# Float8 rounding in units 6 and 7 of a chunk, and the float8 product in unit 0 of the next, in a fused attention block

## The chip, the cores and the metric

The kernel runs on one core of a Trainium2 chip, as a single launch. The metric is device time in microseconds (us), lower is better. The core has a matrix engine (PE, whose weight loads are shown as PEld), a vector engine (DVE), a scalar engine (ACT), a general engine (POOL) and a queue that issues DMAs (SP). Each engine works through its own instructions in order and waits on semaphores for the others.

## What is computed

The input is `x`, 4 batches of 1024 tokens of 512 values, all in float32. It is normalized, and the result is the input plus an attention block plus a small product in float8:

```python
xn = _layernorm(x)
x = x + attention(xn, ...) + ffn(xn, input2, scale, scale1)

# ffn
q1 = (xn * scale).astype(float8_e4m3fn)
q2 = (input2 * scale1).astype(float8_e4m3fn)
out = (q1.astype(float32) / scale) @ (q2.astype(float32) / scale1)

# attention: 16 heads of 128
q = rope(rmsnorm(xn @ Wq + bq)); lk = rope(rmsnorm(xn @ Wlk + blk)); lv = xn @ Wlv + blv
entries = weighted mean of each 4 tokens of xn         # 256 per batch
ck = rope(rmsnorm(entries @ Wk + bk)); cv = entries @ Wv + bv
sparse = softmax over the 8 best of q . ck, times cv    # causal
local  = softmax of q . lk over the 128 tokens before and itself, times lv
out = ((sparse + local) / 2) @ Wo + bo
```

The change touches only when the float8 part `ffn(xn, ...)` is computed.

## The kernel before

**Tiles.** The tokens are cut into 32 chunks of 128 (`t`, 0 to 31; `c = t mod 8` is the chunk's place in its batch). The 16 heads of a chunk are worked in 8 units of two heads (`u`, 0 to 7). The main loop (L791) runs over steps `s = 8 t + u` and in each step works on several units at once: scores and softmax of unit s, queries and keys of unit s + 3, values' projection of unit s + 1, the context of unit s - 1 and the output projection of unit s - 2. The order of every instruction on every engine is the order of the code: it is written by hand, and no scheduler changes it.

**One step on PE** (the order in which it meets its work): `scores` of unit s for two heads (sc, L572 to L583), `queries` (qp, L445 and L446), what the chunk work adds in its first call (below), `to_output` (op, L753), `values_of` (vp, L537), `values` (cp, L720). A little of a name's meaning: qp holds raw queries and keys, th the normalized and rotated ones (L467, L309 to L312), vp the raw values, which ACT copies to lv (L549), prob the softmax weights, which DVE (L661) and DMAs (pr, then probT, L703) transpose.

**One step on DVE**: `weigh` and `settle` of unit s (L605 to L638), the chunk work of the first call, the chunk work of the second call, the add of the output when a chunk ends (L762, in unit 1 of the next chunk), `turn` (L661), `normalize` (L467, L310 to L312), `turn_keys` (L512, L515). On POOL: the chunk work of the first call, the reciprocal root r (L290, L291), the chunk work of the second call, and rb (L309).

**Chunk work** is done by generators, of which each step takes two pieces: the function `steps()` (L768) calls `next` once on every generator in the list `running`, and the main loop calls it twice a step, first after `settle` (L812), then after `to_output` (L818).

- `chunk_prep(t + 2)` (L318) starts in u = 7 of chunk t and takes 18 pieces, nine steps: layernorm (L329 to L337: statistics in unit 7, xn in unit 0), its transposition on PE (xp, L342, unit 1), the projection yp (L352, unit 2), the entries ep (L382, unit 4), kv (unit 5), its scaling and rotation on DVE and POOL (L404, then L309 to L312 for 32 entries, unit 6), the transposition cp on PE (L412) in the first call of unit 7, and its copy to ckT on DVE (L414) in the second call of unit 7. The scores of the next chunk read ckT (L582).
- `chunk_eight(t)` (L417) is the float8 part in six pieces. Piece 1: three DVE operations on 128 x 512 (L262, L263, L266) and a POOL add (L267). Pieces 2 to 4: one POOL operation each (L269, L271, L273), the last of which writes x8. Piece 5: the product on PE, four bfloat16 matmuls into fp (L425). Piece 6: DVE scales fp and adds the bias (f, L430), and POOL adds f to x_sum (L431). In unit 1 of the next chunk L762 adds the attention's output to x_sum, and SP stores it (L763).

In the kernel before, `chunk_eight(t)` starts in u = 5: pieces 1 and 2 in unit 5, pieces 3 and 4 in unit 6, pieces 5 and 6 in unit 7.

**Shared buffers.** All these PSUM tiles come from one tag, `pp`, with two buffers in turn: vp of every unit, and xp, yp, ep, cp and fp of the chunk work. A tile can be written only when the last reader of the tile two before it in the order of the code is done. In unit 7 that order is cp, fp, vp. In the same way xn, y, qv, qm and f share two buffers named `scratch`, and the inputs x two buffers.

## Time and profile before

| | |
|---|---|
| time, median of 3 runs | 2831.97 us (2831.59 to 2832.27) |
| the profiled execution | 2833.53 us, its span 2831.6 us |
| granted PE clock, mean | 0.997 |
| HBM traffic | 140 GB/s over the span |
| one chunk, by the starts of vp | some 80 to 94 us, longer with c |

Share of the span is how long an engine was busy. A matmul's end is modelled and matmuls overlap, so the busy time of PE isn't the time of its stream; the starts of its groups are. In the timeline each line has the start and the length in us, the engine, the line of the code, the operation, what is written and read, the shape and how many of them, and in brackets the idle time just before and what ended it.

The chunk work of the float8 part, with its counts and mean lengths:

```profile
L262 DVE TENSOR_SCALAR qv_x<-xnT,scales 128x512 f32<-128x512 f32 x32 | 15.3, 479 | 0.0
L263 DVE TENSOR_SCALAR qm_x<-qv_x 128x512 uint32<-128x512 uint32 x32 | 13.7, 427 | 1.1
L266 DVE TENSOR_SCALAR qm_x<-qm_x 128x512 f32<-128x512 f32 x32 | 13.7, 427 | 1.1
L267 POOL TENSOR_TENSOR qv_x<-qv_x,qm_x 128x512 f32<-128x512 f32 x32 | 40.7, 1273 | 34.2 <-DVE qm_x L266 34.2
L425 PE MATMUL fp<-w_sb,x 128*128 128x512 bf16 x127 | 32.9, 381 | 0.1
```

The columns after the bar are the busy time in us, the mean length of one in ns, and the idle time before them with what ended it.

### The profile page before, as it was taken

Reading aid. Unit: us, or ns where it says so; the run is one execution under the profiler, and the core shown is the slowest. Engines: PE = TensorE matmul, PEld = TensorE weight load, DVE = VectorE, ACT = ScalarE, POOL = GpSimd, SP = SyncE. Lnnn points to the kernel's source line nnn. Section 1 sums busy time; section 2 is a strip of 40 time slices with the busy share of each in tenths; the row PEclk is TensorE's granted clock in tenths of the full one; section 3 lists DMA queues with packets and bytes.
Section 4 is the critical chain, followed back from the end, with each engine's and each line's share of the span. In section 5 each row is a group of like instructions: output and inputs, shape, how many; then the busy total and the mean of one; then the engine's idle time right before and its main releaser. Section 6 shows DMA issues by size and latency. Waiting matters only on the chain. (4 is left out here: it accounts for less than half of the span.)

```text
span 2831.6 us, 48506 instructions
## 1 busy us (share of the span) xinstructions
PE 2769.0 (98%) x12771; PEld 1873.8 (66%) x12969; DVE 2247.1 (79%) x9132; ACT 1299.1 (46%) x5075; POOL 821.3 (29%) x1161
## 2 busy tenths in 40 slices
PE   6999999999999999999999999999999999999998
PEld 4666666666666666666666666666666666667666
DVE  5777888888777778888877787888887777888886
ACT  3445444444444454444444444444444444444443
POOL 3432232322233322233223333223222233322221
PEclk9999999999999999999999999999999999999999
DMA  7345455555445445555544444555554544555553
GB/s 230 90 138 138 133 143 152 144 150 153 127 124 139 137 133 152 144 151 149 149 126 131 134 135 134 155 148 149 146 149 122 135 136 131 136 152 155 143 149 108
DMA packets 620850, 399.85 MB, mean 141 GB/s; under 512 B 306880, under 2 KB 573984, under 8 KB 620576
## 3 DMA queue, kind: packets, MB, share of 16 engines
q1 hardware_dynamic: 608352, 383.18, 48.8%
q10 hardware_dynamic: 12224, 13.56, 1.5%
q8 instruction: 105, 1.72, 0.3%
q14 instruction: 169, 1.38, 0.2%
HBM read 212.53 MB, written 184.03 MB: 140 GB/s over the span
## 5 line engine op out<-in xcount | busy, mean ns | idle before, releaser
L445 PE MATMUL qp<-wqk,xnT 128*128 128x512 f32 x2048 | 945.5, 604 | 4.9 <-DMA scales<-in_L_ffn_scale_dram 3.3
L445 PEld LDWEIGHTS qp<-wqk,xnT 128*128 128x128 f32 x2048 | 370.6, 191 | 385.2 <-issue 371.5
L612 ACT ACTIVATE prob<-sc,neg 128x256 f32<-128x256 f32 (+1 forms) x512 | 236.0, 461 | 779.6 <-DVE taken L611 759.3
L537 PEld LDWEIGHTS vp<-wlv,xnT 128*128 128x128 f32 x2048 | 386.5, 190 | 188.7 <-issue 94.0
L537 PE MATMUL vp<-wlv,xnT 128*128 128x256 f32 x2048 | 487.0, 381 | 17.2 <-DVE ckT L414 11.9
L753 PE MATMUL op<-wo,cT 128*128 128x512 f32 x1024 | 484.9, 596 | 7.1 <-ACT cT L735 1.5
L290 POOL TENSOR_SCALAR r<-ss 128x4 f32<-128x4 f32 x256 | 49.8, 194 | 1067.3 <-ACT junk L296 1059.3
L661 DVE STREAM_TRANSPOSE probB<-prob 128x512 f32<-128x512 f32 (+2 forms) x494 | 282.4, 609 | 92.5 <-ACT prob L643 89.1
L467 DVE SCALAR_TENSOR_TENSOR th<-qp,r,norm_w 128x128 f32<-128x128 f32 x1024 | 283.6, 339 | 71.0 <-POOL r L291 70.2
L309 POOL TENSOR_TENSOR rb<-th,cs 128x256 f32<-128x256 f32 x256 | 247.0, 965 | 278.0 <-DVE th L467 277.9
L296 ACT ACTIVATE junk<-qp 128x128 bf16<-128x128 f32 x1024 | 284.1, 277 | 88.0 <-remote 42.7
L549 ACT COPY lv<-vp 128x256 f32<-128x256 f32 x256 | 95.5, 373 | 477.6 <-PE cp L720 420.0
L753 PEld LDWEIGHTS op<-wo,cT 128*128 128x128 f32 x1024 | 188.9, 190 | 188.4 <-issue 113.9
L720 PE MATMUL cp<-probT,lv 128*128 128x128 f32 x1920 | 299.4, 276 | 4.4 <-DMA probT<-pr 4.4
L720 PEld LDWEIGHTS cp<-probT,lv 128*128 128x128 f32 x1920 | 276.1, 193 | 18.1 <-issue 5.2
L291 POOL TENSOR_TENSOR r<-r,nhalf 128x4 f32<-128x4 f32 x256 | 259.6, 1014 | 21.4
L720 PE MATMUL cp<-probT,cv 128*128 128x128 f32 x1536 | 256.7, 276 | 0.0
L582 PE MATMUL sc<-ckT,qT 128*128 128x96 f32 (+7 forms) x1024 | 226.5, 303 | 0.0
L643 ACT ACTIVATE prob<-prob,tot 128x256 f32<-128x256 f32 (+1 forms) x512 | 223.0, 484 | 3.6 <-DVE tot L637 3.6
L720 PEld LDWEIGHTS cp<-probT,cv 128*128 128x128 f32 x1536 | 214.3, 193 | 0.0
L605 DVE CUSTOM_DVE_ANT_0 sc<-sc,mask_b 128x256 f32<-128x256 f32 (+1 forms) x512 | 202.6, 396 | 7.2 <-PE sc L583 6.6
L579 PE MATMUL sc<-lkT,qT 128*128 128x128 f32 x1024 | 207.8, 285 | 0.0
(123 smaller groups left out, 3858.3 us busy)
## 6 DMA issues: line engine op xcount, KB each, us to landing
pr<-probB SPq DMA_DIRECT2D x127, 512.0 KB, 2.6
probT<-pr SPq DMA_DIRECT2D x508, 128.0 KB, 2.9
qk<-thb SPq DMA_DIRECT2D x992, 64.0 KB, 2.0
pr<-probB SPq DMA_DIRECT2D x96, 384.0 KB, 2.6
probT<-pr SPq DMA_DIRECT2D x384, 96.0 KB, 2.4
qT<-qk SPq DMA_DIRECT2D x248, 128.0 KB, 2.3
lkT<-qk SPq DMA_DIRECT2D x248, 128.0 KB, 2.5
x_norm<-_attn_hidden_states_dram SPq DMA_DIRECT2D x32, 256.0 KB, 3.2
```

What stands on the lines that cost most here:

```text
L291: nc.gpsimd.tensor_tensor(r, r, nhalf[: ss.shape[0], 0:n], ALU.pow)
L296: nc.scalar.activation(junk[: src.shape[0]], src, AF.Square, accum_out=acc)
L309: nc.gpsimd.tensor_tensor(bb, x12, wide(cs[:, HALF:ROPE]), ALU.mult)
L445: nc.tensor.matmul(qp, xnT[:, k, :], wqk_sb[u][:, k, :], start=(k == 0), stop=False)
L467: nc.vector.scalar_tensor_tensor(th[:, i, :], qp[:, ts(i, D)], r[:, i : i + 1], norm_w[:, i // 2, :], ALU.mult, ALU.mult,)
L537: nc.tensor.matmul(vp[:, 0:256], xnT[:, k, :], wlv_sb[u][:, k, :], start=(k == 0), stop=(k == KK - 1),)
L582: nc.tensor.matmul(sc[:, spa], q, ckT[:, 0:m], start=True, stop=False)
L612: nc.scalar.activation(prob[:, loc], sc[:, loc], AF.Exp, bias=neg[:, 0:1], scale=-1.0, accum_out=tot[:, 0:1],)
L643: nc.scalar.mul(prob[:, loc], prob[:, loc], tot[:, 0:1])
L661: nc.vector.transpose(pb[:, :, ds(h * g, g), :], prob[:, parts[0] * P : (parts[-1] + 1) * P].rearrange("p (g b i) -> p b g i", b=NB, i=BLK),)
L720: nc.tensor.matmul(blocks(cp[:, h, :]), v, probT[:, :, h * len(parts) + i - parts[0], :], start=(i == parts[0]), stop=(i == parts[-1]),)
L753: nc.tensor.matmul(op, cT[:, h, :], wo_sb[u][:, h, :], start=(u == 0 and h == 0), stop=(u == NU - 1 and h == 1),)
```

## The change

One condition of the main loop. `chunk_eight(t)` starts one unit later:

```diff
         if u == 3 and 0 <= t < NT:
             load_x(t, "sum")
-        if u == 5 and 0 <= t < NT:
+        if u == 6 and 0 <= t < NT:
             running = [*running[-2:], chunk_eight(t)]
         if u == 4 and 0 <= t and t + 2 < NT:
             load_x(t + 2, "norm")
```

Pieces 1 and 2 now fall in unit 6, pieces 3 and 4 in unit 7, and pieces 5 and 6 (the product, f and the add to x_sum) in unit 0 of the next chunk, one step before L762 reads x_sum. The order in `running` stays the same: in unit 6 `chunk_prep` comes before `chunk_eight`. The order of the `pp` tiles becomes cp, vp in unit 7 and fp, vp in unit 0; that of `scratch` becomes xn, f, y, qv, qm instead of xn, y, qv, qm, f. For the last chunk pieces 5 and 6 fall in the step after its last unit.

## The prediction

> **What bounds the kernel now.** I read the busy shares first, then the waits, then the timelines of PE, DVE, ACT and POOL around the end of a chunk. I write t for the chunk (0 to 31), c = t mod 8, u for the unit (0 to 7), and x(u7) for the x of unit 7.

> ```profile
> PE 2769.0 (98%) x12771; PEld 1873.8 (66%) x12969; DVE 2247.1 (79%) x9132; ACT 1299.1 (46%) x5075; POOL 821.3 (29%) x1161
> ```

> Of the waits (engine, line, waited for; us in total, times, longest) the two that return:

> ```profile
> PEld vp L537 <- DVE ckT L414: 36.1, 30, 1.9
> ...
> PE vp L537 <- DVE ckT L414: 11.9, 18, 1.1
> ```

> PE runs nearly gaplessly; what shortens PE's stream shortens the kernel. The one wait of PE that returns with every chunk is vp (L537) on the copy of ckT (L414), 30 times. The timeline of PE shows it in u7 of t = 15, with unit 5, free of it, above:

> ```profile
> 1407.29 1.88 PE L753 MATMUL op<-wo,cT 128*128 128x512 f32 x4
> 1409.01 1.89 PE L537 MATMUL vp<-wlv,xnT 128*128 128x256 f32 x8
> ...
> 1429.22 0.24 PE L412 MATMUL cp<-ident,kv 32*128 32x32 f32 x1
> 1429.40 1.04 PE L425 MATMUL fp<-w_sb,x 128*128 128x512 bf16 x4
> 1430.27 1.88 PE L753 MATMUL op<-wo,cT 128*128 128x512 f32 x4
> 1433.20 1.99 PE L537 MATMUL vp<-wlv,xnT 128*128 128x256 f32 x8 [1.05 <-DVE ckT L414]
> ...
> 1437.05 0.32 PE L582 MATMUL sc<-ckT,qT 128*128 128x32 f32 x2
> ```

> From op to vp is 1.72 us in unit 5 and 2.93 here: 1.21 lost. That difference, not the 36.1 (idle weight loads, partly under running matmuls), is the cost. Measured so in the timeline for all 31 chunks with a next one, the excess over 1.72 is 0.00 (t = 0, 1), 0.29, 0.78, 0.13, 0.48, 0.85, 1.21 (t = 2 to 7), then 0.98 at c = 0 and about the same again in each batch: **16.7 us in all**. DVE, same place:

> ```profile
> 1432.17 0.69 DVE L329 BATCH_NORM_STATS2 lnst<-x_norm 128x6 f32<-128x512 f32 x1
> 1432.89 0.18 DVE L330 BATCH_NORM_AGGREGATE lnst<-lnst 128x2 f32<-128x6 f32 x1
> 1432.99 0.16 DVE L414 COPY ckT<-cp 128x32 f32<-128x32 f32 x1
> 1433.06 0.74 DVE L430 SCALAR_TENSOR_TENSOR f<-fp,inv,bo_sb 128x512 f32<-128x512 f32 x1
> ```

> Why vp waits for ckT: all pp tiles share two PSUM buffers, so each waits for the last reader of the tile two before it. In u7 the order is cp, fp, vp: vp takes cp's buffer, freed by L414, which stands behind all of DVE's settling. DVE is late there: weigh starts 0.04 us after its scores in u5 of t = 15, 2.00 in u6, 2.46 in u7, because of the rounding in u5 (L262 to L266, 1.34 us, then 1.30 waiting for POOL's r).

> [...] kv L311 lasts 0.59 us in most of its 32 runs, beside POOL's L271 (0.62), and 0.18 in a few.

> **The change part by part.**

> 1. *fp leaves u7.* Order in u7: cp, vp. vp now takes the buffer of vp(u6), freed by ACT's lv (L549), at 1422.22 in t = 15, ten us earlier. Nothing else of vp is late (xnT is a chunk old). Removed: 16.7 us.

> 2. *fp enters u0* of the next chunk. Its four matmuls cost the same 0.87 us (1429.40 to 1430.27). It waits for cp's buffer (L414, a unit earlier) and for x8 (L273). vp(u0) follows vp(u7), freed by ACT a unit before; xp(u1) follows fp, freed by f (L430) in u0, over 5 us ahead. cp is now followed directly by op; ep before op makes op 0.10 longer (op to vp 1.82 instead of 1.72 in u4), so cp may do the same: 0 to 3.1 us over 31 chunks, taken at 1.5.

> 3. *Rounding DVE work moves from u5 to u6*, behind the kv rotation (L404, L310 to L312, 1.44 us). u5 loses 1.34 and its 1.30 wait for r, so u6 starts about 0 to 0.3 late instead of 2.0. u6 gains L262 to L266 (1.4), and the r wait, since L267 (1.28) now stands before r on POOL: from kv to th was 1.34 and becomes about 1.4 + 2.84. So u6 costs 2.9 more and u7 starts 3.4 to 3.7 late, not 2.46. L271 now follows rb (L309) and meets L311/L312 of th[...]: up to 0.6 more, while kv L311 gets back 0.4. I take 3.9. Cover: nothing on PE needs this until ckT. ckT ends 6.16 after weigh starts, 10.1 after u7's scores; its next reader, L582 of u0, stands 3.85 after vp, or 11.3 after those scores once the stall is gone. **Cover left 1.2 us** at c = 7, about 2 elsewhere, where two other score matmuls come first or the settling is shorter. A microsecond beyond cover costs one microsecond of PE per chunk.

> 4. *POOL.* r, the pow, then one 1.27 us operation, then rb: in u7 L273 takes L431's place, in u6 L269 takes L273's, u0 gains L431, u5 loses L269. x8 ends at 4 (lateness) + 6.1 + 2.3 (lnr, r) + 1.3 = 13.7 after u7's scores; fp comes at 1441.4 - 1.2, 15.7 after: cover 2. No DMA moves; on SP only the readiness of pr and qk shifts, by under 1 us, and from the last probT issue to values the trace has 2.3 us or more.

> 5. *f in u0* adds 0.66 us of issue to DVE. In u0 DVE waits 0.2 to 1.0 for ACT or POOL, and in u1 it waits for op at L762:

> ```profile
> 1453.70 0.69 DVE L762 TENSOR_TENSOR x_sum<-x_sum,op 128x512 f32<-128x512 f32 x1 [2.14 <-PE op L753]
> ```

> These waits (0.75 to 2.14 at L762, then 1.45 or more at L363 in u2) absorb f, the lateness and PE's gain of time; the chain starts anew before u5. Scratch: xn(u0) now follows qv, f follows qm; both are free when L273 ends in u7, some 4 us before xn. Cost 0. L431 (u0) ends some 7 us before L762 (u1).

> 6. *End of the program.* u5 of the last chunk has no rounding any more, so its L661, pr and probT come 1.3 earlier, and PE waits there:

> ```profile
> 2804.80 1.20 PE L720 MATMUL cp<-probT,lv 128*128 128x128 f32 x4 [4.38 <-DMA probT<-pr]
> ...
> 2816.14 0.88 PE L684 MATMUL tp<-ident,prob 128*128 128x128 f32 x4 [0.96 <-DVE f L430]
> ```

> Gain 1.3. The second transposition no longer waits for f (0.5 to 0.6), but fp now waits for ACT's probT copy and delays op by 0.6: together 0. Sum 1.3.

> **Sum.** -16.7 + 1.5 - 1.3 = -16.5. Against the profiled execution: 2833.5 (span 2831.6 and 1.9 around it) - 16.5 = 2817.0. That execution lies 1.6 above the median shown, 2831.97, so on the scale of the median **2815.5**.

> **Rivals.**

> *A, part of the gain comes back* (0.14): ckT or x8 late beyond cover in the later chunks of a batch. For: cover is only 1.2 at c = 7. Against: three batch edges alone give 3 us per us. Half the gain lost: 2824.

> *B, the wait only changes its name* (0.06): vp still meets a late buffer or u0 waits the same time at L582. For: the DVE lateness is moved, not cured. Against: lv ends ten us early. Time: 2832.

> *C, slower* (0.12): rounding on top of kv in u6 makes DVE late to L414. It decides where ckT comes 2 us later than I reckon; slower by 0.2% needs (16.5 + 5.7)/31 = 0.7 us per chunk beyond that. At 2.9 us, 0.9 x 31 = 28 us: 2843. For: u6 and u7 are DVE's fullest units, idle only 0.85 and 1.02 us of 11.4 and 11.9 at t = 15, and two of POOL's operations stand in new company. Against: u5, emptied, starts u6 nearly on time.

> **How the numbers follow.** Forecast 0.68: 2815.5, its own range 2812 to 2820 (op penalty 0 to 3.1, end 0 to 2, a microsecond or so at batch edges). With A the range 2811 to 2829 holds 0.8. This kernel's measurement can tell about 0.2%, 5.7 us: faster if below 2826.3. Forecast and most of A give 0.79 faster; B and the rest of A 0.08 same; C and a little besides 0.13 slower.

> **What would show it.** Right: no line of vp on ckT in the waits; op to vp 1.72 to 1.82 in every u7; fp between qp and op in u0; weigh in u6 nearly on time and in u7 some 3.5 to 4 late. Wrong: PE waiting at L582 on ckT or at L425 on L273 (A, C), or at vp on ACT's lv or on f (B).

## The result and the profile after

The changed kernel takes 2818.39 us (median of 4 runs, 2817.43 to 2818.91) against 2832.09 us before: a ratio of 0.9951, 95% interval 0.9934 to 0.9969. Measured again in a later comparison it took 2814.04 us against 2832.27 (0.9935, 0.9921 to 0.9948), and in a third 2814.50 against 2832.17 (0.9936, 0.9924 to 0.9949). It is 0.5 to 0.65% faster; the forecast was 2815.5. Its first profiled execution has a span of 2816.8 us, 14.8 less than before. All lines of "after" below are of that execution.

Busy times and shares, from the page after:

```profile
span 2816.8 us, 48762 instructions
...
PE 2779.5 (99%) x12969; PEld 1873.5 (67%) x12969; DVE 2244.6 (80%) x9132; ACT 1282.1 (46%) x5075; POOL 815.2 (29%) x1161
```

DVE and POOL do the same instructions as before (9132 and 1161) and are busy for nearly as long. PE's busy time can't be compared, since 198 of its matmuls are missing from the trace of before (12771 of 12969); the starts of its groups can. The gain is idle time of PE. In the list of waits, "vp on ckT", 30 times before, is gone. Three lines are new or have grown (before: 5.2 us in 3 times, 4.4 in 1, and none; "issue" means that the profile shows nothing that ended the wait):

```profile
PEld cp L720 <- issue: 10.0, 13, 4.1
...
PE cp L720 <- DMA probT<-pr: 6.5, 5, 3.7
...
PE sc L582 <- DVE ckT L414: 0.7, 3, 0.4
```

PE's timeline in unit 7 and unit 0 after t = 15, where 1.21 us were lost before:

```profile
1420.30 0.24 PE L412 MATMUL cp<-ident,kv 32*128 32x32 f32 x1
1420.47 1.98 PE L753 MATMUL op<-wo,cT 128*128 128x512 f32 x4
1422.29 1.89 PE L537 MATMUL vp<-wlv,xnT 128*128 128x256 f32 x8
...
1426.04 0.32 PE L582 MATMUL sc<-ckT,qT 128*128 128x32 f32 x2
...
1430.24 0.38 PE L446 MATMUL qp<-bias_b,sel 128*128 128x512 bf16 x1
1430.45 1.03 PE L425 MATMUL fp<-w_sb,x 128*128 128x512 bf16 x4
1431.32 1.88 PE L753 MATMUL op<-wo,cT 128*128 128x512 f32 x4
```

From op to vp is 1.82 us now, in 30 of 31 chunks (1.72 in the first), and fp stands between qp and op of unit 0 with no gap. DVE's timeline at the same place:

```profile
1419.51 0.40 DVE L605 CUSTOM_DVE_ANT_0 sc<-sc,mask_b 128x256 f32<-128x256 f32 x1
...
1425.52 0.16 DVE L414 COPY ckT<-cp 128x32 f32<-128x32 f32 x1
...
1443.55 0.69 DVE L762 TENSOR_TENSOR x_sum<-x_sum,op 128x512 f32<-128x512 f32 x1
```

Read the two together: ckT is copied at 1425.68, 3.39 us *after* vp starts. DVE is later than before and PE no longer cares; ckT's next reader is L582 at 1426.04, so 0.36 us of cover (the time by which ckT is early for its next reader) is left. L762, which before waited 2.14 us for op, has no idle time ahead of it: this wait of DVE has taken up part of its lateness.

Where the 14.8 us went, from the starts of vp in all 256 steps (after less before, profiled executions):

| | us |
|---|---|
| wait of vp in unit 7 (1.72 or 1.82 from op instead of up to 2.93) | -16.6 |
| fp and cp: +0.76 in each unit 0, -0.77 in each unit 7 beyond the wait, 31 times | -0.3 |
| u0 after the first chunk of three batches (c = 0): PE at L582 for ckT (0.42, 0.65, 0.46) | +1.5 |
| nine steps in which values wait for probT (0.09 to 1.0) | +3.5 |
| start of the program and first chunk | -2.5 |
| end of the program | -0.7 |

They sum to -15.1. The 0.4 left is in four u0 (t = 1, 2, 10 and 18) that grew by 0.86 to 0.90 instead of 0.76.

### The profile page after: what moved, and what is told of

Read it like the earlier page. It is cut to its first block, busy times and chain, and to the rows that moved or that the text cites. A ratio compares the mean times of both kernels' runs of the same rounds, so it can differ in the third digit from the quotient of the medians.

```text
span 2816.8 us, 48762 instructions
## 1 busy us (share of the span) xinstructions
PE 2779.5 (99%) x12969; PEld 1873.5 (67%) x12969; DVE 2244.6 (80%) x9132; ACT 1282.1 (46%) x5075; POOL 815.2 (29%) x1161
## 3 DMA queue, kind: packets, MB, share of 16 engines
q8 instruction: 105, 1.72, 0.3%
## 4 chain that ended last, share of the span: by engine, by line
PE 92%; DVE 3%; DMA 1%; POOL 1%; ACT 1%; SPq 0%; issue 0%; ACTq 0%; DVEq 0%; POOLq 0%
PE qp L445 30%; PE op L753 15%; PE vp L537 15%; PE cp L720 13%; PE sc L582 5%; PE sc L572 4%; PE sc L579 4%; PE qp L446 2%; PE yp L352 2%; PE fp L425 1%; DMA pr<-probB 1%; PE ep L382 1%; PE xp L342 0%; DMA probT<-pr 0%; ACT junk L296 0%
## 5 line engine op out<-in xcount | busy, mean ns | idle before, releaser
L537 PEld LDWEIGHTS vp<-wlv,xnT 128*128 128x128 f32 x2048 | 388.8, 190 | 166.9 <-issue 113.1
L537 PE MATMUL vp<-wlv,xnT 128*128 128x256 f32 x2048 | 484.2, 379 | 4.8 <-DVE lkT L497 3.0
L753 PE MATMUL op<-wo,cT 128*128 128x512 f32 x1024 | 488.0, 599 | 0.5 <-ACT cT L735 0.5
L661 DVE STREAM_TRANSPOSE probB<-prob 128x512 f32<-128x512 f32 (+2 forms) x494 | 283.1, 611 | 92.8 <-ACT prob L643 81.5
L309 POOL TENSOR_TENSOR rb<-th,cs 128x256 f32<-128x256 f32 x256 | 245.3, 958 | 269.4 <-DVE th L467 268.3
L720 PE MATMUL cp<-probT,lv 128*128 128x128 f32 x1920 | 299.3, 276 | 6.6 <-DMA probT<-pr 6.5
L753 PEld LDWEIGHTS op<-wo,cT 128*128 128x128 f32 x1024 | 186.4, 190 | 177.9 <-issue 120.5
L720 PEld LDWEIGHTS cp<-probT,lv 128*128 128x128 f32 x1920 | 274.4, 192 | 23.3 <-issue 10.0
L720 PE MATMUL cp<-probT,cv 128*128 128x128 f32 x1536 | 256.1, 276 | 0.0
L582 PE MATMUL sc<-ckT,qT 128*128 128x96 f32 (+7 forms) x1024 | 227.1, 304 | 0.7 <-DVE ckT L414 0.7
L549 ACT COPY lv<-vp 128x256 f32<-128x256 f32 x256 | 94.9, 371 | 276.2 <-PE cp L720 241.6
L720 PEld LDWEIGHTS cp<-probT,cv 128*128 128x128 f32 x1536 | 213.5, 193 | 0.0
L311 DVE TENSOR_TENSOR th<-thb,rb 128x128 f32<-128x128 f32 x256 | 87.2, 341 | 155.7 <-POOL rb L309 155.0
```

The costliest lines, as they stand in the source:

```text
L309: nc.gpsimd.tensor_tensor(bb, x12, wide(cs[:, HALF:ROPE]), ALU.mult)
L537: nc.tensor.matmul(vp[:, 0:256], xnT[:, k, :], wlv_sb[u][:, k, :], start=(k == 0), stop=(k == KK - 1),)
L582: nc.tensor.matmul(sc[:, spa], q, ckT[:, 0:m], start=True, stop=False)
L661: nc.vector.transpose(pb[:, :, ds(h * g, g), :], prob[:, parts[0] * P : (parts[-1] + 1) * P].rearrange("p (g b i) -> p b g i", b=NB, i=BLK),)
L720: nc.tensor.matmul(blocks(cp[:, h, :]), v, probT[:, :, h * len(parts) + i - parts[0], :], start=(i == parts[0]), stop=(i == parts[-1]),)
L753: nc.tensor.matmul(op, cT[:, h, :], wo_sb[u][:, h, :], start=(u == 0 and h == 0), stop=(u == NU - 1 and h == 1),)
```

## The experiments

The theory: PE's gain is the order in which the shared PSUM buffers come free, by the product leaving unit 7. The rival: the rounding's DVE work leaving unit 5 is what pays. A second question was what the moved rounding costs.

**e1: only the product moves.** Rounding in units 5 and 6 as before.

```diff
         if u == 5 and 0 <= t < NT:
             running = [*running[-2:], chunk_eight(t)]
...
         yield from quantize(x8, src, scales[:, 0:1], f"x_{t}")
+        yield
+        yield
         fp = pp(f"fp_{t}")
```

> Rounding stays in units 5 and 6 as before; only the product and f move to unit 0 (two empty pieces before the product). If the gain is the buffer order alone (vp of unit 7 no longer behind cp and fp): op to vp 1.72 to 1.82 in every unit 7 and 2812 to 2816 us, a little below the changed kernel's 2818.4, since DVE is not made later before ckT and x8 is ready two units early: no wait of PE at the product, none at ckT. If the gain came from taking the rounding out of unit 5: about 2832 us.

Measured: 2813.34 us against 2832.44 (0.9935, 0.9923 to 0.9948). The timeline of e1 at t = 15 (the lines of the code are two further on):

```profile
1421.45 0.24 PE L412 MATMUL cp<-ident,kv 32*128 32x32 f32 x1
1421.63 1.98 PE L755 MATMUL op<-wo,cT 128*128 128x512 f32 x4
1423.45 1.89 PE L539 MATMUL vp<-wlv,xnT 128*128 128x256 f32 x8
```

The wait is gone with the rounding where it was. DVE starts weigh 2.00 and 2.48 us late in units 6 and 7 of t = 15, as before the change (2.00, 2.46), so its lateness is no part of the gain. The rival falls.

**e2: the whole float8 part one unit earlier than before**, so that the product is in unit 6. Against the kernel before:

```diff
-        if u == 5 and 0 <= t < NT:
+        if u == 4 and 0 <= t < NT:
```

> The whole float8 part one unit earlier than before: rounding in units 4 and 5, product and f in unit 6. The order of the shared PSUM tiles is then fp, vp in unit 6 and cp, vp in unit 7. Buffer order: the wait on ckT is gone too, 2811 to 2816 us. If it is the later place of the rounding that helps: 2832 us or more, as it goes the other way.

Measured: 2815.35 us against 2832.44 (0.9941, 0.9929 to 0.9954); op to vp 1.82 in unit 7. Moved the other way the change pays as well. What matters is that the product is in another unit than cp.

**e3: all of the rounding in unit 6, product in unit 7.** The generator gives way only after every second piece of the rounding. Against the changed kernel:

```diff
-        yield from quantize(x8, src, scales[:, 0:1], f"x_{t}")
+        for i, _ in enumerate(quantize(x8, src, scales[:, 0:1], f"x_{t}")):
+            if i % 2:
+                yield
```

> All four pieces of the rounding in unit 6 (two in each call), the product again in unit 7, so cp, fp, vp as before. Buffer order: the wait of vp on ckT is back, and longer than before, as DVE reaches unit 7 some 5 us late instead of 2.5: 2 to 3 us in a chunk, 2870 to 2900 us. If moving the rounding is what pays: 2818 to 2832 us.

Measured: 2979.01 us, a ratio of 1.0518 (1.0503 to 1.0532). The direction is as expected, the size is not. PE's timeline of e3 in unit 7 of the same chunk:

```profile
1500.94 1.04 PE L427 MATMUL fp<-w_sb,x 128*128 128x512 bf16 x4
1501.82 1.88 PE L755 MATMUL op<-wo,cT 128*128 128x512 f32 x4
1507.76 3.78 PE L539 MATMUL vp<-wlv,xnT 128*128 128x256 f32 x8 [4.06 <-DVE ckT L414]
```

DVE reaches unit 7 here 5.48 us late and vp waits 4.22 (3.8 in the mean of 30 chunks), and then the eight matmuls of vp take 3.78 us instead of 1.89. The windows around the wait show the clock (after the length: busy us of PE, PEld, DVE, ACT and POOL with their counts, PE's granted clock, DMA share, GB/s):

```profile
1507.70:1509.00 1.30, 1.24 (x3) 1.06 (x4) 1.30 (x4) 0.10 (x1) 1.03 (x4) 0.50 0.00 0
1509.00:1511.00 2.00, 2.00 (x6) 1.53 (x6) 1.61 (x5) 0.00 (x0) 2.00 (x2) 0.50 0.30 123
...
1513.00:1515.00 2.00, 2.00 (x21) 2.00 (x20) 0.90 (x5) 0.63 (x2) 0.00 (x0) 1.00 0.00 0
```

The clock is granted at 0.50 when vp starts and is back at 1.00 some five microseconds later. The expectation took 2 to 3 us of wait for a chunk and no slow clock. The waits came to 115 us in all, against 16.6 before, and the slow vp after them to some 35 more.

**e4: the changed kernel with a spare tile between cp and vp**, to put vp behind ckT again.

```diff
             nc.tensor.transpose(cp[:, 0:NE], ck[:, 0, :], ident[:NE, :NE])
+        spare = pp(f"spare_{t}")
+        nc.tensor.matmul(
+            spare[:, 0:NE], ident_b, mask_b[:, 2 * P : 2 * P + NE], start=True, stop=True
+        )
         yield "A8"
```

> The changed kernel with one more tile of the shared PSUM buffers between cp and vp of unit 7, written by one matmul of 32 columns that nobody reads; its result is not used. vp again takes the buffer that L414 frees. Buffer order: vp waits 1.5 to 3 us in every unit 7, 2870 to 2895 us, slower than before, since DVE is later there than before. If the order of buffers is not the cause: 2818 plus at most 5 us for the matmul.

Measured: 2817.65 us (0.9947, 0.9932 to 0.9963): no wait of vp came back. Taken alone this speaks against the theory, but vp starts 3.3 us before ckT is copied (t = 15), so it can't have taken cp's buffer. The addresses in the program agree: vp got the buffer of the spare tile. The rule "the tile two before it", as the text ahead of the prediction has it, is not exact: a new tile got the buffer whose last use stands earliest in the code, and the spare tile's last use, its own matmul, stands ahead of the copy of ckT. In unit 7 both rules give the same buffers in the kernels before and after. The experiment did not do what it was meant to do.

**e5: the same, but DVE reads the spare tile after ckT**, so that cp's buffer is the one that comes free first.

```diff
         nc.vector.tensor_copy(ckT[:, ts(c, NE)], cp[:, 0:NE])
+        seen = work.tile([P, NE], F32, tag="seen", name=f"seen_{t}", bufs=1)
+        nc.vector.tensor_copy(seen, spare[:, 0:NE])
```

> The changed kernel with a spare tile of the shared PSUM buffers between cp and vp of unit 7 that DVE reads (0.16 us) after it has copied ckT, so that cp's buffer is the one freed first and vp has to take it; the spare's values are not used. In the changed kernel the copy of ckT ends 2.6 us after vp starts, in the mean of the chunks. Buffer order: vp waits that long again in each of 30 chunks, 2880 to 2915 us. If the order of the buffers does not matter: 2818 to 2824 us.

Measured: 2944.44 us against 2832.27 (1.0396, 1.0382 to 1.0410), and 130 us above the changed kernel in the same comparison. From the waits, then PE's and DVE's timelines of e5 after t = 15:

```profile
PE vp L543 <- DVE ckT L418: 85.2, 30, 3.2
```

```profile
1483.52 0.19 PE L414 MATMUL spare<-mask_b,ident_b 128*128 128x32 bf16 x1
1483.56 1.96 PE L759 MATMUL op<-wo,cT 128*128 128x512 f32 x4
1488.76 3.59 PE L543 MATMUL vp<-wlv,xnT 128*128 128x256 f32 x8 [3.23 <-DVE ckT L418]
```

```profile
1488.54 0.16 DVE L418 COPY ckT<-cp 128x32 f32<-128x32 f32 x1
```

vp starts 0.05 or 0.06 us after the copy's end in all chunks but the first. The product is in unit 0 and the rounding in units 6 and 7, as in the changed kernel. e4 has the same extra matmul and no wait of vp, and the extra copy stands behind that of ckT; what differs for vp is the buffer. This shows the mechanism: with the same work ahead of ckT on DVE, the wait is there or not by the buffer that vp takes. The size is again larger than expected. Measured against 1.72 from op to vp, the wait is 3.1 us in the mean (30 chunks, 92 us in all) where 2.6 was reckoned; the changed kernel's trace has 2.96 us in the mean from vp's start to the copy's end, so the 2.6 was too low to begin with. The slow clock (0.984 in the mean of e5's profiled execution, 0.998 in the changed kernel's) adds about 30 us to vp alone.

**e7, and the changed kernel and e1 again: what does the late DVE cost?** After the first runs the changed kernel seemed 5 us behind e1. e7 keeps the rounding's DVE work in unit 5 and writes x8 only in unit 7.

```diff
-        yield from quantize(x8, src, scales[:, 0:1], f"x_{t}")
+        for i, _ in enumerate(quantize(x8, src, scales[:, 0:1], f"x_{t}")):
+            yield
+            if i == 1:
+                yield
+                yield
```

> Rounding's DVE operations and its first two POOL operations in unit 5 as before, its last two POOL operations in unit 7 and the product in unit 0 as in the changed kernel. If the 5 us by which the changed kernel is behind e1 come from DVE being late in units 6 to 0: 2813 to 2815 us, no wait of PE for the product. If they come from x8 being written only in unit 7: 2815 to 2818 us, with PE waiting at the product after each chunk at the head of a batch.

> The changed kernel itself, beside the two below on one chip: 2817 to 2820 us.

> The kernel of e1 once more, on the chip of the changed kernel: 2812 to 2815 us, 4 to 6 us below it.

Measured in one comparison: the changed kernel 2814.04 us (2812.90 to 2815.89), e1's order 2814.25 (2812.67 to 2814.49), e7 2812.28 (2812.02 to 2813.80). Here the 5 us were not there. A third comparison of the same three, with what was expected of the changed kernel, of e1's order and of e7's:

> The changed kernel a third time, beside the two below on one chip. So far 2818.4 and 2814.0 us. If DVE's lateness costs PE some 3 to 5 us in waits for probT and ckT whatever the chip: 3 to 5 us above the kernel below. If that cost hangs on how fast the DMAs of pr land: near it where they land in 2.7 us, above it where they need 3.0.

> Rounding in units 5 and 6, product in unit 0, a third time: 2812.5 to 2815 us on any chip, since no wait of PE for probT or ckT is left in it.

> Rounding's DVE work in unit 5, last two POOL operations in unit 7, product in unit 0, once more: 2811.5 to 2814 us, at or up to 2 us below the kernel above (its DVE is about 0.2 us less late in unit 7).

Measured: 2814.50, 2813.64 and 2813.34 us. Side by side the changed kernel is -0.2 and +0.9 us from e1's order, less than these runs can tell. The waits do stay: PE at L582 for ckT three times in each profile of the changed kernel, and probT waits of a number that goes with the DMA of pr. In the first profile a 512 KB pr took 3.0 us to land (median) and weight loads of L720 sat idle 13 times; in the second and third it took 2.7 and 2.8 us, and they sat idle 8 and 6 times. In e1's and e7's profiles it is 3 or 4 times, nearly all of the idle time at the end of the program. That the slower landing made the first comparison 4 us higher fits these three profiles, but it was not varied by itself and stays open. On the chip of the first experiments such a gap did show side by side: e4, which is the changed kernel and one small matmul, took 2816.09 to 2819.18 us there against e1's 2812.84 to 2814.95, with a pr of 2.9 us and the same waits for probT and ckT. The second and third comparison ran on another chip, so what the late DVE costs may depend on the chip. e7 has the lowest median in both later comparisons, but its range overlaps the others', so there no version is shown to beat the changed kernel.

## Why the prediction was right, step by step

1. *fp leaves u7*: right, in mechanism and size. 16.7 us of op-to-vp excess were counted before (16.6 in the table above), and none is left but the 0.10 per chunk of point 2. e5 shows the cause by giving it back, e1 by taking it alone. DVE's lateness, which made the wait long, needed no cure.
2. *fp enters u0*: the penalty of cp ahead of op is real, 0.10 in each of 30 chunks, the upper end of what was allowed. But something was left out of the sum. fp itself costs the 0.87 that was reckoned (1430.45 to 1431.32), and still u0 grew by only 0.76 in most chunks: a vp that had waited was followed by PE's next group 1.83 us after its start, one that had not waited 1.73 after it. This 0.10, in 27 chunks, takes back most of what cp costs, so both together are -0.3 us, not +1.5.
3. *Rounding on top of kv in u6*: weigh in u7 of t = 15 was to be 3.9 us late; it is 3.91, but u6 starts 0.58 late where 0 to 0.3 was said and adds 3.3 where 3.6 was reckoned, so that the sum fits so well is in part luck. The meeting of L271 with th L311, priced at up to 0.6 as an estimate from kv L311 (29 of 32 times at 0.59 us before, each beside L271), is there: L311 lasts 0.69 us in 31 of 256 where it lasts 0.29 otherwise, and kv L311 is at 0.18 in all 32. DVE and POOL of the changed kernel at the end of unit 6 of t = 15:

```profile
1417.89 0.69 DVE L311 TENSOR_TENSOR th<-thb,rb 128x128 f32<-128x128 f32 x1 [0.62 <-POOL rb L309]
```

```profile
1417.83 0.62 POOL L271 TENSOR_SCALAR qm_x<-qv_x 128x512 f32<-128x512 f32 x1
```

   What the step got wrong is the cover. It said 1.2 us at c = 7 and about 2 elsewhere; in the first profile 0.36 is left at c = 7, 0.33 at c = 3, and 0.65 to 1.23 in most other chunks. And the tightest place is c = 0, where units are short and DVE is 5.2 to 5.4 late: there the cover is used up at three chunks, and rival A's wait at L582 comes, for 1.5 us in all:

```profile
1503.94 0.45 PE L582 MATMUL sc<-ckT,qT 128*128 128x64 f32 x2 [0.38 <-DVE ckT L414]
```

4. *POOL*: x8 is ready in time. In the trace L273 ends 1.3 us or more before PE reaches fp in every chunk, where 2 was reckoned. What the step said of DMAs was wrong. The margin of 2.3 us was taken from the last issue of probT's DMAs, whose landing still has to come, and pr shifts by more than 1 us: in unit 1 of t = 23 DVE's transposition is later, and pr is issued 6.65 us before vp starts instead of 9.21. In unit 5 of t = 10 the transposition ends 9.18 us before vp in both kernels, and pr is issued 5.80 before it instead of 9.15: in the profile of the changed kernel SP's issues of qT, lkT and x_norm, ahead of that of pr, started only at 949.50, 949.92 and 950.47, after a wait of 1.3 us for qk, and pr's at 951.07. The waits cost 3.5 us in the first profile, 2.4 in the second and 0.8 in the third.
5. *f in u0*: cost nothing on PE. L762 has lost its wait in all chunks but the last, and by unit 5 weigh starts 0.0 to 0.6 us after its scores again (1.0 to 1.1 at c = 0, 2.0 in the first chunk, as before).
6. *The end*: 0.7 us gained where 1.3 was said. The sum also had no term for the start: there 2.5 us went. Of these 1.2 are in the first steps, which differ from profile to profile with the loads of the weights; the other 1.3 to 1.4 are in units 6 and 7 of the first chunk, and are missing from e1's profile, so they come from the rounding's leaving unit 5. That DVE reached unit 6 of this chunk 4.46 us late before, and 1.31 now, fits this.

So the term that was right carries the result. Small terms of the sum were off or missing, by 1 to 4 us each, and partly cancel: cp (1.5 too little), the group after vp (-2.7, left out), ckT and probT (taken at nothing), the start (-2.5, left out). The three medians, 2814 to 2818, lie on both sides of the forecast; that it came so close to them is in part luck.

Of the rivals, A came true in small: ckT is late beyond cover after c = 0, for 1.5 us and not for half the gain. B falls by the profile, in which no wait has taken the place of the old one, and C by the time itself. What C feared does exist: in e3 and e5 the kernel is 147 and 112 us slower than before, because vp's buffer hangs on the late DVE.

## What to carry to other kernels

When a tile of the bottleneck engine waits in one place of a loop for a busy engine, list which tiles share its buffers and in which order their last uses stand in the code: moving one tile out of that place can cure the wait without making any engine faster. Before moving the work of the engine that is late, compute how long its next reader can wait in the *shortest* unit of the loop, not in the busiest, and count a DMA's margin from its landing. And test a buffer theory by giving the wait back, with a tile that is sure to take the buffer in question: a spare tile that nobody reads doesn't hold one.

## What the runs showed of the hardware

In e5 a wait of PE often cost more than itself. Of its 30 waits in unit 7 (each measured as the excess of op to vp over 1.72 us), the four of 2.7 us were followed by vp at its usual length (1.83 us to the next group). But 21 of the 25 of 2.8 to 3.5 us, and the shortest, of 2.5 us at t = 30, were followed by vp at 2.6 to 3.6 us. The waits of the kernel before, up to 1.21 us, were never followed by a slow vp (at most 1.83 us to the next group). So in e5 the length of a wait did not decide alone.

```profile
567.01:570.42 3.41, 2.18 (x6) 0.83 (x6) 3.17 (x18) 2.20 (x10) 0.00 (x0) 1.00 0.72 178
570.42:573.83 3.41, 1.79 (x8) 1.61 (x9) 2.77 (x9) 1.71 (x8) 1.58 (x4) 1.00 0.40 91
...
1294.05:1297.46 3.41, 1.04 (x5) 0.93 (x6) 3.27 (x12) 2.42 (x11) 0.91 (x3) 1.00 0.40 89
1297.46:1300.87 3.41, 3.41 (x14) 3.06 (x13) 1.81 (x7) 0.00 (x0) 3.25 (x4) 0.50 0.38 154
```
